# The mLSTM of a two-layer block: sums in four column groups of TensorE, state in row groups

## The chip, the cores and the metric

The kernel runs on one core of a Trainium2 chip, as one launch. The metric is the device time in microseconds, the median of several runs. A core has five engines that matter here: TensorE (PE in the profile, with its weight loads shown apart as PEld), VectorE (DVE), ScalarE (ACT), GpSimd (POOL) and SyncE (SP, which issues DMAs). Each engine works through its own list of instructions in order and waits on semaphores for the others.

## The reference

The input x has 4 sequences of 512 positions and 256 features. Layer 0 adds to x, both computed from the layer norm of x, an xLSTM block (an mLSTM and an MLP of 1024) and an FFN of 704 with low-rank experts. Layer 1 adds an attention and a sparsified FFN. Everything is in 32-bit floats. The change touches the mLSTM alone. It has 8 heads, with queries and keys of 16 and values of 32 numbers:

```python
logfg = jax.nn.log_sigmoid(f_pre)
Fcum = jnp.cumsum(logfg, axis=-1)
Dmat = Fcum[..., :, None] - Fcum[..., None, :] + i_pre[..., None, :]
Dmat = jnp.where(causal, Dmat, -jnp.inf)
m = jnp.max(Dmat, axis=-1, keepdims=True)
Smat = jnp.exp(Dmat - m)
qk = jnp.einsum('bhsd,bhtd->bhst', q, k) / jnp.sqrt(jnp.float32(dqk))
C = qk * Smat
n = jnp.maximum(jnp.abs(jnp.sum(C, axis=-1, keepdims=True)), jnp.exp(-m))
h = jnp.einsum('bhst,bhtd->bhsd', C / n, v)
```

So for every position two sums over the earlier positions are wanted, with the same weights C: the sum of C times the values (32 numbers a head) and the sum of C itself (one number a head).

## The kernel before

The 512 positions are cut into four stages j of 128 positions, all four sequences b together. The sum over earlier positions is split: within the stage it is computed from C, and what came before is carried in a state (key times value, summed over positions, faded from stage to stage). Each stage's mLSTM (`mlstm(j)`, L643) goes through these steps:

- Queries and keys come as 128 rows (8 heads of 16) by 512 columns (4 sequences of 128 positions).
- **h_ps** (L700, stages 1 to 3): what the old state gives. For each b, one matrix product with the queries as stationary operand (128 by 128) and the state of b as moving operand: 8 heads of 33 numbers, 264 columns. Each head uses only the rows of its own 16; the rest of the state is kept at zero by the mask `own_head`. ACT copies it to `hr`, positions on the partitions.
- **pass_on** (L786, stages 0 to 2) is the making of the new state: keys are transposed (`kt_ps`), and for each b one product `st_ps` of keys (stationary, 128 by 128) with weighted values (264 moving columns). DVE masks it with `own_head` and adds it to the state, which POOL has faded (L834).
- **ct** holds the exponents: for each head parity s, a tile [128 source positions, 4 head pairs r, 4 sequences of 128 target positions], so head 2r + s. It comes by DMA, POOL masks it, DVE subtracts, ACT takes the exponential.
- **qk** (L852): queries times keys, each in a row group of 32 rows of TensorE's array, four heads at once, each into its own PSUM bank; DVE multiplies it into `ct`, which is then C transposed.
- **weighted** (L814) is the sum within the stage. For each head and b one product **hp**: C of 128 by 128 as stationary operand, and as moving operand the 33 columns of `va`, 32 of the values and one with a factor, which gives the sum of C. DVE adds it to `hr`. There are 32 such products in a stage: 8 heads by 4 sequences.
- After that `hr` is normalised (L886 on) and goes through the output projection.

Every 32-bit product is two records in the profile, each a weight load and a matmul; a transpose is one record.

What runs when is set while the program is built. The generators (`experts`, `mlp`, `mlstm`, `routing` and so on) are streams. A planner (`Clock` L51, `Flow` L223) keeps an estimate of when each tile is ready and when each engine is free, and at each step lets the stream go on whose next product is ready; `flow.wait` names tiles and the number of free PSUM banks needed, `banks=4` for four. The order that comes of this is fixed in the program for every engine. So around the steps of the mLSTM stand products of the FFN (chunk, acc, gp, up, yp), and a change of one step moves others. All engine calls go through one helper, so nearly every row of the profile shows line L216, and rows are told apart by their tiles. `mm(..., at_once=4)` (L293) only tells the planner that four such products run side by side.

## Time and profile before

| | |
|---|---|
| median of 3 runs | 789.7 us (789.66 to 790.86) |
| the profiled execution, its own time | 789.78 us |
| its span, first to last instruction | 788.1 us, granted TensorE clock 1.000 |
| PE busy | 774.3 us (98%), 3334 records |
| DVE, ACT, POOL busy | 404.1, 265.1, 167.5 us |
| hp, h_ps, st_ps on PE | 256, 24, 24 records |

The span is what the trace covers; 1.7 us of the execution lie outside it. A PE record's duration in a group reaches from its start to the end of its result, and records overlap, so what a product costs a full engine is the distance from its start to the next start. A timeline row gives the first start, the time to the last end and the count of a run of equal records.

### The profile page before, as it was taken

Reading aid. Unit: us, or ns where it says so; the run is one execution under the profiler, and the core shown is the slowest. Engines: PE = TensorE matmul, PEld = TensorE weight load, DVE = VectorE, ACT = ScalarE, POOL = GpSimd, SP = SyncE. Lnnn points to the kernel's source line nnn. Section 1 sums busy time; section 2 is a strip of 40 time slices with the busy share of each in tenths; the row PEclk is TensorE's granted clock in tenths of the full one; section 3 lists DMA queues with packets and bytes.
Section 4 is the critical chain, followed back from the end, with each engine's and each line's share of the span. In section 5 each row is a group of like instructions: output and inputs, shape, how many; then the busy total and the mean of one; then the engine's idle time right before and its main releaser. Section 6 shows DMA issues by size and latency. Waiting matters only on the chain.

```text
span 788.1 us, 8741 instructions
## 1 busy us (share of the span) xinstructions
PE 774.3 (98%) x3334; PEld 531.5 (67%) x3334; DVE 404.1 (51%) x933; ACT 265.1 (34%) x473; POOL 167.5 (21%) x156
## 2 busy tenths in 40 slices
PE   6999999999999999999999999999999999999998
PEld 3687787867757787674778775656645485764487
DVE  4566545674331775432246532311278784836980
ACT  3536316471112564303146212011243405135310
POOL 5230250600240330140021031000333303233000
PEclk9999999999999999999999999999999999999999
DMA  8820001200000300000030121001000000000000
GB/s 257 268 95 1 0 1 36 73 1 1 0 1 0 109 1 1 1 1 0 0 108 1 44 75 44 0 1 53 0 1 0 1 27 1 1 27 1 0 22 33
DMA packets 18970, 25.37 MB, mean 32 GB/s; under 512 B 2800, under 2 KB 12784, under 8 KB 18928
## 3 DMA queue, kind: packets, MB, share of 16 engines
q1 hardware_dynamic: 17408, 24.39, 9.7%
q10 hardware_dynamic: 1520, 0.43, 0.2%
q8 instruction: 26, 0.43, 0.2%
q14 instruction: 16, 0.13, 0.1%
HBM read 22.65 MB, written 2.16 MB: 31 GB/s over the span
## 4 chain that ended last, share of the span: by engine, by line
PE 97%; ACT 1%; DMA 1%; DVE 0%; issue 0%
PE chunk L216 20%; PE yp L216 18%; PE gp L216 14%; PE up L216 14%; PE acc L216 11%; PE qk_ps L216 3%; PE hp L216 3%; PE vp L216 2%; PE pt L216 2%; PE o_ps L216 2%; PE lp L216 2%; PE v_ps L216 2%; PE qk L216 1%; PE k_ps L216 1%; PE q_ps L216 1%; PE h_ps L216 1%
## 5 line engine op out<-in xcount | busy, mean ns | idle before, releaser
L216 PE MATMUL chunk<-low,lora 128*128 128x256 f32 (+1 forms) x384 | 87.6, 385 | 1.6 <-DVE hid L216 1.0
L216 ACT ACTIVATE sl<-chunk 128x256 f32<-128x256 f32 x132 | 48.4, 385 | 107.7 <-PE chunk L216 98.9
L216 PE MATMUL chunk<-xnT,wguT 128*128 128x256 f32 (+1 forms) x384 | 84.2, 383 | 0.0
L216 PEld LDWEIGHTS chunk<-xnT,wguT 128*128 128x128 f32 (+1 forms) x384 | 63.6, 181 | 19.0 <-issue 7.4
L216 PEld LDWEIGHTS chunk<-low,lora 128*128 128x128 f32 (+1 forms) x384 | 63.0, 181 | 16.7 <-issue 4.8
L216 ACT ACT_TABLE_LOAD x46 | 59.0, 1283 | 11.4 <-DMA wvg<-in_WrT 6.1
L216 PE MATMUL gp<-featT,w_gate 128*128 128x512 f32 x128 | 60.3, 593 | 0.0
L216 PE MATMUL gp<-xnT,wguT 128*128 128x512 f32 x128 | 60.2, 592 | 0.0
L216 PE MATMUL up<-featT,w_up 128*128 128x512 f32 x128 | 60.2, 592 | 0.0
L216 PE MATMUL up<-xnT,lora 128*128 128x512 f32 x128 | 60.1, 592 | 0.0
L216 DVE TENSOR_TENSOR hid<-up,tmp 128x512 f32<-128x512 f32 x32 | 22.1, 692 | 72.7 <-PE up L216 70.0
L216 PE MATMUL yp<-w_down,hid 128*128 128x256 f32 x256 | 56.2, 379 | 0.0
L216 PE MATMUL yp<-w_gate,hs 128*128 128x256 f32 x256 | 56.2, 379 | 0.0
L216 PEld LDWEIGHTS yp<-w_down,hid 128*128 128x128 f32 x256 | 48.5, 190 | 8.2 <-issue 1.7
L216 PEld LDWEIGHTS yp<-w_gate,hs 128*128 128x128 f32 x256 | 48.6, 190 | 6.6
L216 ACT ACTIVATE tmp<-gp 128x512 f32<-128x512 f32 x32 | 19.1, 598 | 94.1 <-PE gp L216 94.1
L216 DVE TENSOR_TENSOR x<-yp,x 128x512 f32<-128x512 f32 (+1 forms) x18 | 11.4, 632 | 67.5 <-PE yp L216 67.5
L216 PEld LDWEIGHTS up<-xnT,lora 128*128 128x128 f32 x128 | 24.2, 190 | 29.3 <-issue 28.2
L216 PEld LDWEIGHTS up<-featT,w_up 128*128 128x128 f32 x128 | 24.2, 190 | 27.9 <-issue 27.3
L216 PEld LDWEIGHTS gp<-featT,w_gate 128*128 128x128 f32 x128 | 24.1, 190 | 27.9 <-issue 27.0
L216 PEld LDWEIGHTS gp<-xnT,wguT 128*128 128x128 f32 x128 | 24.1, 190 | 27.9 <-issue 27.3
L216 PE MATMUL acc<-WdT,hid 128*128 128x256 f32 (+1 forms) x192 | 41.5, 386 | 0.0
(198 smaller groups left out, 1209.4 us busy)
## 6 DMA issues: line engine op xcount, KB each, us to landing
ct<-m_dram SPq DMA_DIRECT2D x8, 1024.0 KB, 8.0
x<-in_x SPq DMA_DIRECT2D x3, 512.0 KB, 9.8
out<-x SPq DMA_DIRECT2D x6, 256.0 KB, 2.1
w_gate<-in_w_gate SPq DMA_DIRECT2D x1, 1024.0 KB, 6.7
w_up<-in_w_up SPq DMA_DIRECT2D x1, 1024.0 KB, 8.1
w_down<-in_w_down SPq DMA_DIRECT2D x1, 1024.0 KB, 11.2
wguT<-in_f_gate SPq DMA_DIRECT2D x1, 1024.0 KB, 5.0
lora<-in_f_up SPq DMA_DIRECT2D x1, 1024.0 KB, 4.8
```

What stands on the lines that cost most here:

```text
L216: return tc.keep_in_program_order(f(*args, **kw))
```

## The change

Two things are done to the mLSTM of layer 0.

The sums within the stage change operands. The values (32 columns of one head) become the stationary operand, in one of four column groups of the array, one for each head pair r; C becomes the moving operand, 128 columns. The result `hv` has head pair and value on the partitions and the target position along the row. The column with the factor is no longer part of it: a second set of products, `sums`, has as stationary operand 32 columns of the tile `ones_at`, zero but for one column at place s, so that the sums of all 8 heads of all sequences gather in one bank over both parities. ACT copies the three banks (two `hv`, one `sums`) into free parts of `ct`; `tok`, 12 transposes a stage, brings them back to positions on partitions, and DVE adds these three to `hr`.

The state is kept by row groups of two heads: 32 rows, with the values of two heads (66 columns) for each b, and the mask `parity` in place of `own_head`. `h_ps` is then 16 products a stage in four row groups, into four banks (`banks=4`), `st_ps` 16 products in four column groups, into one bank. One POOL instruction fades the whole state, with a factor that two small DVE instructions (`own`, `fade`) choose for each row; one DVE instruction masks it and one adds it.

```diff
-        state = [new(wk0, [P, H, DV + 1], f"state{b}") for b in range(B)]
+        state = new(wk0, [P, B, 2, DV + 1], "state")
+        ones_at = new(sm, [P, B, 2 * DV], "ones_at")
+        pool.memset(ones_at, 0.0)
...
             if not first:
+                yield from flow.wait(qs, state, banks=H // 2)
+                hps = [mm_ps("h_ps") for _ in range(H // 2)]
                 for b in range(B):
-                    yield from flow.wait(qs, state[b], banks=1)
-                    h_ps = mm_ps("h_ps")
-                    mm(h_ps[:, 0:W], qs[:, cols_of(b)], state[b].rearrange("p h d -> p (h d)"),
-                       start=True, stop=True)
-                    act.copy(hr[:, b, :, :], by_head(h_ps[:, 0:W]))
+                    for r, h_ps in enumerate(hps):
+                        mine = slice(32 * r, 32 * r + 32)
+                        mm(h_ps[:, b * W2 : (b + 1) * W2], qs[mine, cols_of(b)],
+                           state[mine, b, :, :].rearrange("p i d -> p (i d)"), start=True,
+                           stop=True, at_once=4)
+                for r, h_ps in enumerate(hps):
+                    act.copy(hr[:, :, 2 * r : 2 * r + 2, :],
+                             h_ps[:, 0 : B * W2].rearrange("p (b i d) -> p b i d", b=B, i=2))
...
+                st_ps = mm_ps("st_ps")
                 for b in range(B):
-                    mm(st_ps[:, 0:W], k_tok[:, b, :], wvs[b].rearrange("p h d -> p (h d)"),
-                       start=True, stop=True)
-                    dve.tensor_tensor(
-                        state[b] if first else wvs[b], by_head(st_ps[:, 0:W]), own_head, ALU.mult)
+                    for r in range(H // 2):
+                        mine = slice(32 * r, 32 * r + 32)
+                        mm(st_ps[mine, b * W2 : (b + 1) * W2], k_tok[:, b, mine],
+                           wvs[b][:, 2 * r : 2 * r + 2, :].rearrange("p i d -> p (i d)"),
+                           start=True, stop=True, at_once=4)
+                dve.tensor_tensor(
+                    new_state, st_ps[:, 0 : B * W2].rearrange("p (b i d) -> p b i d", b=B, i=2),
+                    parity.unsqueeze(1).unsqueeze(3).to_broadcast([P, B, 2, DV + 1]), ALU.mult)
...
-            def weighted(s, r):
-                hp = mm_ps("hp")
-                for b in range(B):
-                    mm(hp[:, b * (DV + 1) : (b + 1) * (DV + 1)], ct[s][:, r, cols_of(b)],
-                       va[:, b, 2 * r + s, :], start=True, stop=True)
...
+            def by_columns(out, lhsT, s, start, stop):
+                for b in range(B):
+                    for r in range(H // 2):
+                        mm(out[32 * r : 32 * r + 32, cols_of(b)], lhsT(b, r),
+                           ct[s][:, r, cols_of(b)], start=start and b == 0, stop=stop,
+                           at_once=4, skip_group_check=True)
+            def to_tokens(n):
+                yield from flow.wait(hvT[n], banks=1)
+                tok = mm_ps("tok")
+                for b in range(B):
+                    transpose(tok[:, cols_of(b)], hvT[n][:, cols_of(b)], ident)
...
+            for s in range(2):
+                yield from flow.wait(ct[s], banks=1 if sums else 2)
+                hv = mm_ps("hv")
+                by_columns(hv, lambda b, r: va[:, b, 2 * r + s, 0:DV], s, True, True)
+                if not sums:
+                    sums = mm_ps("sums")
+                    clock.held.add(sums.tensor.name)
+                by_columns(sums, lambda b, r: ones_at[:, b, DV - s : 2 * DV - s], s, s == 0, s == 1)
+                act.copy(hvT[s], hv)
+                if s == 1:
+                    act.copy(hvT[2], sums)
+                    clock.held.discard(sums.tensor.name)
+            for n in range(3):
+                yield from to_tokens(n)
```

The order of the changed program shows, in each of the four stages: both `qk` blocks, some products of the FFN, then `hv`, `sums`, `hv`, `sums` as one unbroken block of 64 products, then the three groups of `tok`, with products of the FFN between them in stages 0 and 2 and next to each other in stages 1 and 3.

More of the change, by code (lines that the diff above doesn't have):

```diff
@@ L403, in layers_kernel @@
     )
-    own_head = new(const, [P, H, DV + 1], "own_head")
-    nc.gpsimd.memset(own_head, 1.0)
-    for base, step in ((0, -DQK), (DQK - 1, DQK)):
+    own_pair = new(const, [P, H // 2], "own_pair")
+    nc.gpsimd.memset(own_pair, 1.0)
+    for base, step in ((0, -2 * DQK), (2 * DQK - 1, 2 * DQK)):
         nc.gpsimd.affine_select(
-            out=own_head, in_=own_head, pattern=[[step, H], [0, DV + 1]], compare_op=ALU.is_ge,
+            out=own_pair, in_=own_pair, pattern=[[step, H // 2]], compare_op=ALU.is_ge,
             fill=0.0, base=base, channel_multiplier=1 if step < 0 else -1)
@@ L475, in layers_kernel @@
         HB = H * B
-        W = H * (DV + 1)
+        W2 = 2 * (DV + 1)
         def tmp():
@@ L772, in mlstm @@
             carry["all"] = m_all
+            if sub_n is not None:
+                own = new(sm, [P, B, 2, H // 2], "own")
+                dve.tensor_tensor(
+                    own, dec[:, sub_n, :, :].rearrange("p (r i) b -> p b i r", i=2),
+                    own_pair.unsqueeze(1).unsqueeze(1).to_broadcast([P, B, 2, H // 2]), ALU.mult)
+                fade = new(sm, [P, B, 2], "fade")
+                dve.tensor_reduce(fade, own, AX.X, ALU.add)
             def spread_dec(n, b):
@@ L793, in pass_on @@
                 act.copy(k_tok, kt_ps.rearrange("p (b c) -> p b c", c=P))
+                yield from flow.wait(*wvs, k_tok, banks=1)
+                st_ps = mm_ps("st_ps")
                 for b in range(B):
-                    yield from flow.wait(wvs[b], k_tok, banks=1)
-                    st_ps = mm_ps("st_ps")
-                    mm(st_ps[:, 0:W], k_tok[:, b, :], wvs[b].rearrange("p h d -> p (h d)"),
-                       start=True, stop=True)
-                    dve.tensor_tensor(
-                        state[b] if first else wvs[b], by_head(st_ps[:, 0:W]), own_head, ALU.mult)
+                    for r in range(H // 2):
[3 more added lines that the diff above has]
+                           start=True, stop=True, at_once=4)
+                new_state = state if first else wvs[0].rearrange("p (b i) d -> p b i d", b=B)
+                dve.tensor_tensor(
+                    new_state, st_ps[:, 0 : B * W2].rearrange("p (b i d) -> p b i d", b=B, i=2),
+                    parity.unsqueeze(1).unsqueeze(3).to_broadcast([P, B, 2, DV + 1]), ALU.mult)
                 while not first and not faded:
                     yield flow.soon()
-                for b in range(B):
-                    if not first:
-                        yield from flow.wait(state[b])
-                        yield flow.spare()
-                        dve.tensor_tensor(state[b], state[b], wvs[b], ALU.add)
+                if not first:
+                    yield from flow.wait(state)
+                    yield flow.spare()
+                    dve.tensor_tensor(state, state, new_state, ALU.add)
                 passed.add(j)
@@ L811, in mlstm @@
                 flow.add(pass_on(), 1)
-            def weighted(s, r):
-                hp = mm_ps("hp")
-                for b in range(B):
-                    mm(hp[:, b * (DV + 1) : (b + 1) * (DV + 1)], ct[s][:, r, cols_of(b)],
-                       va[:, b, 2 * r + s, :], start=True, stop=True)
-                got = hp[:, 0 : B * (DV + 1)].rearrange("p (b d) -> p b d", b=B)
-                to = hr[:, :, 2 * r + s, :]
-                if first:
-                    dve.tensor_copy(to, got)
-                else:
-                    dve.tensor_tensor(to, got, to, ALU.add)
             for s in range(2):
@@ L833, in mlstm @@
             if not first:
-                for t, n in ((hr, old_n), (state, sub_n))[: 1 if last else 2]:
-                    for b in range(B):
-                        mine = t[b] if t is state else hr[:, b, :, :]
-                        pool.tensor_tensor(out=mine, in0=mine, in1=spread_dec(n, b), op=ALU.mult)
-                        yield flow.soon(0.6)
+                for b in range(B):
+                    mine = hr[:, b, :, :]
+                    pool.tensor_tensor(out=mine, in0=mine, in1=spread_dec(old_n, b), op=ALU.mult)
+                    yield flow.soon(0.6)
+                if not last:
+                    by_row = state.rearrange("p b i d -> p (b i) d")
+                    pool.tensor_tensor(
+                        out=by_row, in0=by_row, in1=fade.rearrange("p b i -> p (b i)").unsqueeze(
+                            2).to_broadcast([P, 2 * B, DV + 1]), op=ALU.mult)
                 faded.add(j)
@@ L849, in mlstm @@
                 act.activation(ct[s], ct[s], AF.Exp, scale=-1.0)
+            dve.tensor_copy(ones_at[:, :, DV], rr[:, 0, :])
+            sums = None
+            hvT = [ct[0][:, 2, :], ct[0][:, 3, :], ct[1][:, 0, :]]
+            def by_columns(out, lhsT, s, start, stop):
[7 more added lines that the diff above has]
+                tok = mm_ps("tok")
+                for b in range(B):
+                    transpose(tok[:, cols_of(b)], hvT[n][:, cols_of(b)], ident)
+                tok = tok.rearrange("p (b r d) -> p b r d", b=B, d=DV)
+                heads = hr.rearrange("p b (r s) d -> p b r s d", s=2)
+                if n < 2:
+                    got, to = tok, heads[:, :, :, n, 0:DV]
+                else:
+                    got, to = tok[:, :, :, 0:2], heads[:, :, :, :, DV]
+                if first:
+                    dve.tensor_copy(to, got)
+                else:
+                    dve.tensor_tensor(to, got, to, ALU.add)
             for s in range(2):
@@ L859, in mlstm @@
                     dve.tensor_tensor(ct[s][:, r, :], qk, ct[s][:, r, :], ALU.mult)
-                for r in range(H // 2):
-                    yield from flow.wait(ct[s][:, r, :], banks=1)
-                    weighted(s, r)
-                    yield flow.soon(0.4)
+            for s in range(2):
[12 more added lines that the diff above has]
+                yield from to_tokens(n)
             if first:
```

## The prediction

> **What bounds the kernel now.** I read the page's busy times first, then its chain, then who waits on TensorE.

> ```profile
> PE 774.3 (98%) x3334; PEld 531.5 (67%) x3334; DVE 404.1 (51%) x933; ACT 265.1 (34%) x473; POOL 167.5 (21%) x156
> ...
> PE   6999999999999999999999999999999999999998
> ...
> PE 97%; ACT 1%; DMA 1%; DVE 0%; issue 0%
> ```

> A busy PE is not yet a PE at its peak, but the chain that ended last is PE for 97% of the span. The list of PE's waits confirms it:

> ```profile
> PE pt L216 <- DVE xn L216: 5.8, 2, 5.6
> PE hp L216 <- DVE ct L216: 1.5, 2, 0.8
> PE vp L216 <- ACT xnT L216: 1.5, 1, 1.5
> PE chunk L216 <- DVE hid L216: 1.0, 2, 0.8
> PE chunk L216 <- DVE tmp L216: 0.6, 1, 0.6
> ```

> That is almost all of it: 10.6 us, of which 7.3 belong to the first 9 us. So the kernel is a queue of TensorE products with other work hidden behind it: what is saved on PE comes off the end, and what is saved elsewhere is worth nothing unless PE waits for it.

> **What a product costs.** This I take from start to next start, in the PE timeline.

> ```profile
> 36.08 0.60 PE L216 MATMUL kt_ps<-ident,kT 128*128 128x128 f32 x4
> 36.52 1.89 PE L216 MATMUL chunk<-xnT,wguT 128*128 128x256 f32 x8
> 38.25 1.94 PE L216 MATMUL st_ps<-wv,qs 128*128 128x264 f32 x8
> 40.03 1.89 PE L216 MATMUL chunk<-low,lora 128*128 128x256 f32 x8
> ```

> Full array: 256 moving columns cost 1.73/8 = 0.216 us a record, 264 columns 1.78/8 = 0.223, a transpose 0.44/4 = 0.109. So a moving column costs 0.84 ns, and 128 of them 0.107 us.

> ```profile
> 22.29 1.95 PE L216 MATMUL chunk<-xnT,wguT 128*64 128x256 f32 x16
> ...
> 63.83 0.59 PE L216 MATMUL acc<-tmp,lora 128*128 128x512 f32 x1
> 64.35 1.17 PE L216 MATMUL qk<-qm,kT 32*128 32x128 f32 x32
> 66.29 1.08 PE L216 MATMUL hp<-va,ct 128*128 128x33 f32 x8 [0.76 <-DVE ct L216]
> 67.20 1.19 PE L216 MATMUL vp<-wvg,xnT 128*128 128x280 f32 x4
> 68.23 0.97 PE L216 MATMUL hp<-va,ct 128*128 128x33 f32 x8
> 69.04 2.13 PE L216 MATMUL vp<-wvg,xnT 128*128 128x280 f32 x8
> ```

> hp: 8 records from 66.29 to 67.20 and from 68.23 to 69.04, 0.91 and 0.81 us, 0.10 to 0.11 a record though only 33 columns move (28 ns): the load of 128 stationary columns is the price.
> qk, four row groups: 32 records in 1.17 us, the last lasting 0.27, so 0.90 from the first start to the last. That is 8 rounds of four; the first round also pays a load of weights that nothing hides (0.1), and a round costs 0.80/7 = 0.114, by single records 0.111. Four products thus take the time of one of 128 columns: four really run at once.
> Two column groups (first row, 128 rows by 64 columns): last record 0.38 long, 1.57 us for 7 intervals of two products, 0.224: again the time of one.
> Changing the tiling of the array: the one acc before qk takes 0.52, while 512 columns take 0.43 (q_ps, two in 0.86). So 0.09 to enter, the same to leave (h_ps before a two-column chunk: 8 records 1.88, less 8 x 0.223), and the first load uncovered, 0.1 for 128 stationary columns, about 0.03 for 32.

> **The change part by part.** *Removed on PE.* hp: 128 products, 256 records, 32 groups of 8 at 0.81 to 0.91, mean 0.83: 26.6 us. h_ps and st_ps: 24 records each at 0.223: 5.35 + 5.35. The two waits for ct before hp, 1.5: they come because each hp group follows its qk at once; in the new order products lie between. Together 38.8 us.

> *Added on PE.* hv and sums: 128 products each, 512 records, in rounds of four: 128 rounds. Each moves 128 columns and loads four times 32. No row shows four column groups; the bounds are 0.107 (all four at once, loads hidden) and 4 x 0.107 = 0.43 (one after the other). Nearest rows are qk (four tiles, other direction) and the two-column chunk (this direction, two tiles); both come out at the time of one. I take 0.111: 14.2 us. sums costs as much as hv, though it brings one number a head.
> tok: 48 transposes at 0.109: 5.2.
> h_ps: 96 records, 24 rounds; 66 columns move (55 ns), but 128 stationary columns are loaded as in qk: 0.111, 2.7 us.
> st_ps: 24 rounds of 66 moving and 32 stationary columns, between 0.055 (moving) and 0.111; I take 0.062, near the moving bound since the load is short: 1.5.
> Changes of tiling: four blocks of hv at 0.12 in and 0.2 out, three of st_ps likewise, three of h_ps at about 0.33 (two of them run into a two-column chunk): 1.3 + 1.0 + 1.0 = 3.3.
> Together 26.9 us, so 11.9 less.

> [...]

> [...] Here four row groups give 4 x 0.107/0.111 = 3.86. [...]

> *Other engines, hidden.* DVE loses 32 additions or copies of hr (mean 0.295, 9.4 us) and 20 state instructions (0.43, 8.6); it gains 8 of 128x512 from PSUM (0.69, like hid from up), 5 on the state, 12 tiny ones of about 0.2: some 8 less. POOL loses 8 fades of 0.636 and gains 2. ACT gains 12 copies of 0.59, 7 us on an engine busy 34%. No DMA is added or moved. All this lies behind PE's 98% and counts nothing.

> *New waits.* The second hv needs all of the second ct. In stage 0, the tightest, two chunk products follow qk (1.0 us with the change of tiling), then 0.12, then hv and sums of the first parity, 16 rounds or 1.8 us: PE arrives 3.0 us after the last qk start. DVE's four multiplications end 2.8 us after it (they took 2.48 from 0.28 on). In the other stages 1.7 to 3.4 us of products lie between. tok waits for ACT: the third group comes 1.1 us after the last sums (0.2 out of tiling, eight transposes), the copy needs 0.3 + 0.6. So both are covered, with about 0.2 to spare; if DVE or ACT is behind with FFN work, each stage waits that long, up to some 1 us. Behind a waiting hv stand the FFN products of the same queue. I allow 0.2 in all.

> **The sum.** Profiled span 788.1 - 11.9 + 0.2 = 776.4; the execution was 1.7 longer, 789.78, which is the median but for 0.1: 789.7 - 11.7 = 778.0.

> **The rivals.**
> [...]
> (2) *Waits in place of work*: hv late on DVE's ct, tok on ACT, in all stages 0.5 to 1.2 us each, 2 to 5 given back: 780 to 783. For it: the margins above; before, hp waited twice for ct. Against: DVE and ACT have slack there, and PE waited for little else.
> (3) *Two column groups at once at most, slower than before*: here four different moving streams of 128 rows each have to be read, and the row shows two. A round then costs 0.222, 152 rounds 16 us more: 794. The change breaks even at 11.7/152 = 77 ns over my value, 0.188 a round. Against: four row groups show no such limit, but they read a quarter of the rows each.
> (4) *The change does not do what it says*, the products fall apart into single ones: the built order has them round after round, hv and sums as one block of 64 a stage, so only the array itself can do this; that is (3) or worse.

> **How the numbers follow.** The forecast 68% (its own range 776 to 780), (1) 13%, (2) 11%, (3) and (4) 7%, a rest of 1%. The range 775.5 to 785 holds the forecast, (2) and most of (1), and leaves out (3). Within 0.2% (1.6 us, about what a measurement of this kernel can tell from no change) lies only a narrow strip between (1) and (3): 2%. Faster 90%, slower 8%.

> **What would show it.** [...] tok 0.109 a transpose. h_ps and st_ps under 1 us a stage against 1.8 before. PE's waits: no hp; hv for ct or tok for ACT each under 0.5 in sum; if over 2, it is (2). PE busy about 764. The granted clock stays 1.0. A wait of PE in the FFN or in layer 1 that is not there now would make the prediction wrong in a way that I have not priced.

## The result, and the profile after

| | before | after |
|---|---|---|
| median, six executions each | 790.3 us (789.66 to 790.86) | 785.12 us (784.47 to 786.74) |
| profiled execution, its span | 789.78, 788.1 us | 784.47, 782.6 us |
| granted TensorE clock | 1.000 | 0.996 |

The ratio is 0.9938 (95% interval 0.9925 to 0.9951). The change makes the kernel 5.2 us faster, where 11.7 were forecast.

The page of the kernel after, its busy times, two rows of its slices and its chain:

```profile
PE 765.3 (98%) x3782; PEld 516.3 (66%) x3782; DVE 397.7 (51%) x906; ACT 270.1 (35%) x485; POOL 166.2 (21%) x151
...
PE   6999999999999998999999999999999999999998
...
PEclk9999999999999998999999999999999999999999
...
PE 92%; DVE 3%; ACT 2%; issue 1%; DMA 1%; ACTq 0%; DVEq 0%
```

PE's busy time fell by 9.0 us, but the chain is no longer PE from end to end: 97% became 92%, and DVE and ACT stand in it with 5% where there was 1. And one slice (the sixteenth, 293 to 313 us) has an 8 in both rows: there PE had gaps, and there its clock was not full. PE's waits (engine and tile, what it waited for: us in all, times, the longest):

```profile
PE pt L216 <- DVE xn L216: 5.8, 2, 5.6
PE chunk L216 <- DVE tmp L216: 5.6, 4, 3.7
PE vp L216 <- ACT xnT L216: 1.4, 1, 1.4
PE vp L216 <- DVE tmp L216: 0.8, 1, 0.8
```

The first and third are those of before. hp's 1.5 us are gone, and so is most of the wait for `hid`; in their place PE waits for DVE's `tmp` 5.6 us instead of 0.6, of which one wait is 3.7.

**The products themselves.** PE timeline of the kernel after (first start, time to the last end, records): a `st_ps`, the block of `hv` and `sums` in stage 0, and an `h_ps`.

```profile
37.75 0.67 PE L216 MATMUL st_ps<-wv,qs 128*32 128x66 f32 x32
38.35 1.99 PE L216 MATMUL chunk<-low,lora 128*128 128x256 f32 x8
...
75.57 1.08 PE L216 MATMUL hv<-ct,va 128*32 128x128 f32 x32
76.47 1.06 PE L216 MATMUL sums<-ct,ones_at 128*32 128x128 f32 x32
77.34 1.06 PE L216 MATMUL hv<-ct,va 128*32 128x128 f32 x32
78.22 1.06 PE L216 MATMUL sums<-ct,ones_at 128*32 128x128 f32 x32
79.20 0.66 PE L216 MATMUL tok<-ident,ct 128*128 128x128 f32 x4
...
129.29 1.12 PE L216 MATMUL h_ps<-state,qs 32*128 32x66 f32 x32
130.34 1.99 PE L216 MATMUL chunk<-xnT,wguT 128*128 128x256 f32 x8
```

From 75.57 to 79.20 are 3.63 us for 32 rounds of four: 0.113 with the way in and out of the tiling, 0.109 from round to round by single records. Four column groups on the same rows do run at once, with their loads hidden (a round takes 0.109, 128 moving columns alone 0.107). A `st_ps` takes 0.60, an `h_ps` 1.05.

**Where the time went.** I gave every PE record the time from its start to the next start, waits included, and summed it by tile in both traces. The mLSTM's products: 37.9 us before (hp 27.1, h_ps 5.5, st_ps 5.3), 25.8 after (hv 7.1, sums 7.4, tok 5.4, h_ps 3.2, st_ps 2.7, in which 0.87 is a wait of the product behind it). That is 12.2 less, by the unrounded sums. All other products together take 6.8 *more*, though none was added: chunk from `low` alone 7.2, acc from `tmp` 0.9, while qk lost 0.75 (1.67 less, since hp's waits had counted there, and 0.92 more, of which below). So the saving was made, and over half of it was lost again in FFN products that the change doesn't touch.

**The place.** The PE timeline of the kernel after in stage 2; the last bracket is the idle time before the group and what ended it:

```profile
289.96 1.89 PE L216 MATMUL chunk<-xnT,wguT 128*128 128x256 f32 x8
291.70 1.13 PE L216 MATMUL chunk<-low,lora 128*128 128x256 f32 x4
296.56 2.08 PE L216 MATMUL chunk<-low,lora 128*128 128x256 f32 x4 [3.73 <-DVE tmp L216]
298.57 2.09 PE L216 MATMUL qk<-qm,kT 32*128 32x128 f32 x32
300.59 1.65 PE L216 MATMUL acc<-tmp,lora 128*128 128x512 f32 x2
```

PE stands still for 3.73 us. Afterwards four chunk records take 2.01 us to the next start (0.96 in the rows of other places, with the change of tiling), qk 2.02 instead of 1.10, the two acc 1.58 instead of some 0.95: another 2.6 us. The reason for the second part is in the windows (a stretch, its length, busy time of PE, PEld, DVE, ACT and POOL, granted clock, DMA):

```profile
294.50:295.00 0.50, 0.00 (x0) 0.00 (x0) 0.00 (x0) 0.50 (x1) 0.00 (x0) 0.86 0.00 0
295.00:295.50 0.50, 0.00 (x0) 0.00 (x0) 0.00 (x0) 0.50 (x1) 0.00 (x0) 0.50 0.00 0
297.00:301.00 4.00, 4.00 (x37) 2.94 (x37) 0.32 (x1) 0.38 (x1) 0.00 (x0) 0.50 0.02 4
...
301.50:302.00 0.50, 0.50 (x2) 0.00 (x0) 0.50 (x2) 0.00 (x0) 0.00 (x0) 0.81 0.00 0
```

The clock is granted at half from 294.86 (0.36 us of that slice at 1.0, the rest at 0.5, gives 0.86) to 301.69, 6.83 us.

What PE waited for stands in ACT's timeline at the same place:

```profile
290.48 0.66 ACT L216 ACTIVATE sl<-chunk 128x256 f32<-128x256 f32 x2
291.15 1.28 ACT L216 ACT_TABLE_LOAD   x1
292.45 1.91 ACT L216 ACTIVATE ct<-ct 128x2048 f32<-128x2048 f32 x1
294.37 1.28 ACT L216 ACT_TABLE_LOAD   x1
295.67 1.21 ACT L216 ACTIVATE sl<-chunk 128x256 f32<-128x256 f32 x4
```

The chain of the experts' FFN is chunk on PE, `sl` on ACT, `tmp` on DVE, the second half of chunk on PE. Between two `sl` stands here the exponential of the mLSTM's second `ct`, with a load of a function table before it and one after it: 1.28 + 1.91 + 1.28 = 4.5 us in which ACT gives the FFN nothing. Before, ACT had the same hole, and PE had work in it:

```profile
292.50 1.28 ACT L216 ACT_TABLE_LOAD   x1
293.79 1.91 ACT L216 ACTIVATE ct<-ct 128x2048 f32<-128x2048 f32 x1
295.73 1.28 ACT L216 ACT_TABLE_LOAD   x1
297.02 1.22 ACT L216 ACTIVATE sl<-chunk 128x256 f32<-128x256 f32 x4
```

```profile
292.70 1.02 PE L216 MATMUL acc<-tmp,lora 128*128 128x512 f32 x2
293.56 1.89 PE L216 MATMUL chunk<-xnT,wguT 128*128 128x256 f32 x8
295.28 1.89 PE L216 MATMUL chunk<-low,lora 128*128 128x256 f32 x8
```

So the theory: the planner, given a shorter mLSTM, lays the streams differently against each other; in stage 2 the products that would have covered ACT's hole had been issued already, PE runs dry, and the idle stretch also costs the full clock. A count of the records in the two traces agrees. When ACT's hole begins (292.50 before, 291.15 after), PE has issued 252 records of chunk from `low`, 264 of chunk from `xnT` and 44 of acc from `tmp` in the kernel before, but 260, 278 and 48 in the kernel after. Those 26 records are some 6.5 us of PE's work (an estimate from 0.216 a chunk and 0.43 an acc), more than the hole's 4.5. That this lead is what emptied the queue is argued from the count, not shown by a run.

### The profile page after: what moved, and what is told of

It is laid out like the page before. It is cut to its first block, busy times and chain, and to the rows that moved or that the text cites. A ratio compares the mean times of both kernels' runs of the same rounds, so it can differ in the third digit from the quotient of the medians.

```text
span 782.6 us, 9629 instructions
## 1 busy us (share of the span) xinstructions
PE 765.3 (98%) x3782; PEld 516.3 (66%) x3782; DVE 397.7 (51%) x906; ACT 270.1 (35%) x485; POOL 166.2 (21%) x151
## 4 chain that ended last, share of the span: by engine, by line
PE 92%; DVE 3%; ACT 2%; issue 1%; DMA 1%; ACTq 0%; DVEq 0%
PE yp L216 18%; PE chunk L216 17%; PE up L216 14%; PE gp L216 14%; PE acc L216 10%; PE qk_ps L216 4%; PE vp L216 2%; PE pt L216 2%; PE v_ps L216 2%; PE o_ps L216 2%; PE lp L216 2%; ACT L216 1%; PE qk L216 1%; PE hv L216 1%; PE sums L216 1%
## 5 line engine op out<-in xcount | busy, mean ns | idle before, releaser
L216 PE MATMUL chunk<-low,lora 128*128 128x256 f32 (+1 forms) x384 | 89.3, 389 | 6.1 <-DVE tmp L216 5.6
L216 ACT ACTIVATE sl<-chunk 128x256 f32<-128x256 f32 x132 | 48.5, 385 | 107.6 <-PE chunk L216 90.0
L216 PE MATMUL chunk<-xnT,wguT 128*128 128x256 f32 (+1 forms) x384 | 84.4, 384 | 0.0
L216 PEld LDWEIGHTS chunk<-low,lora 128*128 128x128 f32 (+1 forms) x384 | 63.0, 182 | 23.9 <-DVE tmp L216 7.0
L216 PEld LDWEIGHTS chunk<-xnT,wguT 128*128 128x128 f32 (+1 forms) x384 | 63.6, 181 | 22.1 <-issue 9.2
L216 DVE TENSOR_TENSOR hid<-up,tmp 128x512 f32<-128x512 f32 x32 | 22.1, 692 | 84.3 <-PE up L216 77.8
L216 PE MATMUL up<-featT,w_up 128*128 128x512 f32 x128 | 60.2, 592 | 0.0
L216 PE MATMUL gp<-xnT,wguT 128*128 128x512 f32 x128 | 60.2, 592 | 0.0
L216 PE MATMUL up<-xnT,lora 128*128 128x512 f32 x128 | 60.2, 592 | 0.0
L216 PE MATMUL gp<-featT,w_gate 128*128 128x512 f32 x128 | 60.1, 592 | 0.0
L216 PE MATMUL yp<-w_gate,hs 128*128 128x256 f32 x256 | 56.2, 379 | 0.0
L216 ACT ACTIVATE tmp<-gp 128x512 f32<-128x512 f32 x32 | 19.1, 597 | 107.3 <-PE gp L216 107.3
L216 PE MATMUL yp<-w_down,hid 128*128 128x256 f32 x256 | 56.1, 379 | 0.0
L216 PEld LDWEIGHTS yp<-w_down,hid 128*128 128x128 f32 x256 | 48.6, 190 | 8.3 <-issue 1.4
L216 PEld LDWEIGHTS yp<-w_gate,hs 128*128 128x128 f32 x256 | 48.6, 190 | 6.6
L216 DVE TENSOR_TENSOR x<-yp,x 128x512 f32<-128x512 f32 (+1 forms) x18 | 11.3, 630 | 66.6 <-PE yp L216 66.6
L216 PEld LDWEIGHTS up<-xnT,lora 128*128 128x128 f32 x128 | 24.2, 190 | 29.3 <-issue 28.2
L216 POOL TENSOR_TENSOR pd<-k,q 128x256 f32<-128x256 f32 (+3 forms) x16 | 25.2, 1574 | 83.2 <-ACT k L216 83.2
L216 PEld LDWEIGHTS gp<-xnT,wguT 128*128 128x128 f32 x128 | 24.1, 190 | 27.9 <-issue 27.3
L216 PEld LDWEIGHTS gp<-featT,w_gate 128*128 128x128 f32 x128 | 24.2, 190 | 27.6 <-issue 27.0
L216 PEld LDWEIGHTS up<-featT,w_up 128*128 128x128 f32 x128 | 24.0, 190 | 27.8 <-issue 27.0
```

Source lines behind the costliest of these rows:

```text
L216: return tc.keep_in_program_order(f(*args, **kw))
```

## The experiments

The theory says that the products' saving of some 12 us is there in any order, and that the rest is order and clock. Its rivals: the new products themselves slow down what runs beside them, so that the loss comes back wherever the order is moved; or one of the two parts of the change carries it. In the text below, "front" is the work that opens the next stage (layer norm `xn`, its transposes `pt`, `vp`, keys and queries), which `following` starts.

**The front later, in both kernels.** The due time at which the planner starts the next stage's front is moved; no computation changes.

```diff
         def following(j):
-            yield flow.soon(30)
+            yield flow.soon(36)
```

> The changed kernel, but the next stage's front (layer norm, transposes, vp) starts 36 us after the stage instead of 30; every instruction is kept, only their order moves, so that other products stand where TensorE waited 3.9 us at 292. Theory A (the products cost what was forecast; 7 us were lost in that one wait and in the half clock of 6.8 us behind it): 785.1 - 3.9 - 2.7 = 778.5, 777 to 780.5, granted clock 1.000, no wait of PE for DVE's tmp over 1.5 us after the first 10 us. Theory B (ACT and DVE can't keep up with the shorter PE queue; the wait only moves): 783 to 786, with 4 us or more of such waits elsewhere.

> The kernel before, with the same later front and nothing else. Theory A: it has no long wait to remove, so the time stays within 1.5 us of 790. Theory C (a later front is better whatever the mLSTM does, and has nothing to do with the change): 783 to 786.

Measured: after with the later front 783.07 us (781.29 to 784.26), ratio to before 0.9909 [0.9891, 0.9928]; before with the later front 790.02 (789.3 to 790.89), ratio 1.0000 [0.9991, 1.0009]. The order as such is worth nothing to the kernel before and 2 us to the one after, less than the full recovery that the theory set at 778.5; the time lies in the range of theory B, which said that the wait only moves, though not with B's 4 us of such waits (2.0 for `tmp` in all). In the trace (of the fastest execution, 781.29) the wait at 292 is gone, the mLSTM's products are 13.0 down, but 4.5 are lost elsewhere, the longest single piece in one new wait (PE timeline of after with the later front):

```profile
149.69 0.55 PE L216 MATMUL pt<-ident,xn 128*128 128x128 f32 x3
151.92 0.77 PE L216 MATMUL pt<-ident,xn 128*128 128x128 f32 x5 [1.69 <-DVE xn L216]
```

Moving the order closed one hole and opened another. That speaks for order, but doesn't yet exclude the first rival.

**Each part alone.** One kernel has only `hv`, `sums` and `tok`, with the state as before; the other only the state by row groups, with hp as before.

```diff
# columns alone: before, with
-                for r in range(H // 2):
-                    yield from flow.wait(ct[s][:, r, :], banks=1)
-                    weighted(s, r)
+            for s in range(2):
+                yield from flow.wait(ct[s], banks=1 if sums else 2)
+                by_columns(hv, lambda b, r: va[:, b, 2 * r + s, 0:DV], s, True, True)
...
# state alone: after, with
-                by_columns(hv, lambda b, r: va[:, b, 2 * r + s, 0:DV], s, True, True)
...
+                for r in range(H // 2):
+                    yield from flow.wait(ct[s][:, r, :], banks=1)
+                    weighted(s, r)
```

> The kernel before with the first part alone: hv, sums and tok in place of hp; the state as before (own_head is stored once a head and broadcast, to make room). Forecast's own terms: 28.1 off, 20.7 on, so 7.4 less than before: 783, if its order holds no wait over 2 us. Theory A: 782 to 785, hv and sums 0.111 a round. Theory D (the column groups cost more than they show in their own rows, through contention with the FFN): 787 or more.

> The kernel before with the second part alone: state, h_ps and st_ps in row and column groups; hp as before. The products alone: 10.7 off, 6.2 on, 785.8. Its order has, near 293, the same shape as the changed kernel's (chunk products with nothing ready between them). Theory A: there PE waits about 4 us and loses its full clock again, 789.5 to 792.5, so no gain. Theory E (the wait comes from hv and tok): 785 to 787, no such wait.

Columns alone: 785.26 us (784.62 to 786.27), ratio 0.9940 [0.9925, 0.9955]. Its products are 7.1 down and everything else 2.9 up, without a loss of clock; 2.3 above the 783 expected, just beyond the range given. State alone: 795.77 (795.13 to 796.14), ratio 1.0071 [1.0056, 1.0086], *slower* than before, and outside what was expected, though its products are 5.7 down as they should be. The other products are 11.8 up. PE timeline of the state alone:

```profile
150.59 0.33 PE L216 MATMUL pt<-ident,xn 128*128 128x128 f32 x1 [0.31 <-DVE xn L216]
152.60 0.77 PE L216 MATMUL pt<-ident,xn 128*128 128x128 f32 x5 [1.69 <-DVE xn L216]
...
304.11 2.07 PE L216 MATMUL chunk<-low,lora 128*128 128x256 f32 x4 [3.73 <-DVE tmp L216]
```

It has the very wait of the full change (3.73, for `tmp`, and four chunk records that take 2.07 us together behind it, 2.08 in after) *and* the one at 150, there with 3.4 us at half clock. This kernel has no `hv`, `sums` or `tok`, so these don't make the wait: as far as it blames them, the first rival falls. The state's own products are left to suspect.

**The state alone, with the later front.** The same edit of one number on that kernel.

> The second part alone (state in row and column groups) with the later front; same instructions as the run of the second part alone, other order. Theory A (that run lost its 5.7 us of products and 6 us more to two waits with half clock): 790.3 - 5.7 + 0 to 2 = 784.6 to 786.6. Theory F (the row and column groups of the state disturb something that follows them in any order): 790 or more.

788.34 us (785.84 to 790.28), ratio 0.9977 [0.9962, 0.9992]: 7.4 us back from an edit of order. In the trace the other products are 2.1 up in place of 11.8, so the state's products in themselves don't slow what stands beside them. The median still lies above the 784.6 to 786.6 of theory A. The ten executions form two groups, five at 785.84 to 787.25 with clock 1.000 and five at 789.43 to 790.28 with 0.996 (the profiled one is of the first). What dropped the clock in the others no trace shows.

**Keep PE busy in the hole.** The order of after stays, and where PE would wait at 292, 16 products (32 records) with 128 columns of `ones_at` that are all zero are added into a bank that is still open. The edit sits where the planner finds no product ready, so it had left this stretch idle itself. The zeros change no sum and leave the wait for `tmp` as it is. If idle time costs only itself, this gains nothing.

```diff
         def idle(self, t, why=""):
             if t > self.now:
+                if 290.4 < self.now < 291.5 and self.open is not None and not self.warmed:
+                    self.warmed = True
+                    for _ in range(16):
+                        pe.matmul(self.open[:, 0:P], ident, ones_at[:, :, 0:DV], start=False,
+                                  stop=False, skip_group_check=True)
...
+                    flow.open = dps[half] if c < last - 1 else None
```

> The changed kernel in its own order, with 16 products of zeros (128 moving columns, 3.5 us by the transposes' and hp's pitch) added to an open acc bank in the wait of 3.9 us near 292; they add zero and come while PE waits anyway. Theory A1 (the half clock of 6.8 us follows from the idle TensorE): the wait stays, the clock stays 1.000, 785.1 - 2.7 = 782.4, 781.5 to 783.5. Theory A2 (the clock falls for another reason): 784.5 to 786, clock 0.996 again.

782.26 us (782.1 to 782.97), ratio 0.9902 [0.9888, 0.9917]: 2.9 us faster than after, by adding work. PE timeline and one window of this kernel:

```profile
292.95 3.73 PE L216 MATMUL acc<-ones_at,ident 128*128 128x128 f32 x32
296.85 1.13 PE L216 MATMUL chunk<-low,lora 128*128 128x256 f32 x4 [0.16 <-DVE tmp L216]
297.91 1.17 PE L216 MATMUL qk<-qm,kT 32*128 32x128 f32 x32
```

```profile
296.50:303.30 6.80, 6.64 (x54) 4.20 (x53) 4.72 (x12) 1.19 (x5) 0.00 (x0) 1.00 0.01 2
```

The chunk starts at the same place behind `tmp`, the four records now take 1.06 to the next start in place of 2.01, and qk 1.10 in place of 2.02. So the half clock comes from PE's idling, and costs 2.9 of the 6.8.

**How much idling is enough?** The same kernel with 8 and with 4 such products, so that 2 and 3 us of the wait stay empty.

> As the run with 16 products of zeros in the wait near 292, but with 8: they end 1.9 us after the wait begins, so TensorE is idle for 2.0 us in place of 3.9. Theory G (the full clock is lost only by an idle stretch near 3 us or longer): clock 1.000 and 782 to 783 in every execution. Theory H (about 2 us are enough when they fall badly): some executions near 782.3 at clock 1.000 and some near 785 at 0.996.

> The same with 4 products of zeros: 3.0 us idle are left. Theory G: the clock falls in every execution or in most, 784.5 to 786.5. Theory H: most executions fall, 784.5 to 786.5, some stay at 782.5.

With 8: 782.39 us (781.91 to 783.54), ratio 0.9904 [0.9889, 0.9918], the clock 1.000 in all four executions. With 4: 785.27 (782.28 to 786.0), ratio 0.9931 [0.9909, 0.9953]; three of the four at 0.996 to 0.997, one (782.28) at 1.000. The chunk behind the wait, of the one with 8 and then of the one with 4:

```profile
298.11 1.13 PE L216 MATMUL chunk<-low,lora 128*128 128x256 f32 x4 [1.95 <-DVE tmp L216]
```

```profile
297.68 2.08 PE L216 MATMUL chunk<-low,lora 128*128 128x256 f32 x4 [2.84 <-DVE tmp L216]
```

1.95 us of idling was free of the penalty in four executions of four, 2.84 in one of four, 3.73 in none of the six of after.

**Both edits of the order together.** If ACT's hole is what PE runs into, the two exponentials of a stage can be put together, so that one pair of table loads serves both. With the later front this was expected to bring the forecast's time.

```diff
-            yield flow.soon(30)
+            yield flow.soon(36)
...
                         c, c, g.unsqueeze(3).to_broadcast([P, 2, B, P]), ALU.subtract)
-                yield from flow.wait(ct[s])
+            yield from flow.wait(*ct)
+            for s in range(2):
                 act.activation(ct[s], ct[s], AF.Exp, scale=-1.0)
```

> The changed kernel with the later front (36 us), and both exponentials of a stage's ct one after the other on ACT, once both tiles are ready, so that Silu work isn't stopped twice by two table loads; every other instruction is kept. Theory A (the products save 12 us; what was given back is waits that the order of the streams makes): 790.3 - 12.2 + 0 to 1.5 = 778 to 779.6, PE's waits after the first 10 us no more than before's 3 us, clock 1.000. Theory B (the shorter queue can't be fed): 782 to 785.

778.38 us (777.97 to 778.46), ratio 0.9851 [0.9836, 0.9865]: the fastest of all, 6.7 us below after. Its waits of PE, but for those of before:

```profile
PE vp L216 <- DVE ct L216: 0.8, 1, 0.8
PE chunk L216 <- DVE tmp L216: 0.6, 1, 0.6
PE chunk L216 <- DVE he_pair L216: 0.3, 1, 0.3
...
PE hv L216 <- DVE ct L216: 0.2, 1, 0.2
```

The wait for `tmp` is at the 0.6 of before, the clock at 1.000, the mLSTM's products 12.1 down, all others 0.7 up. ACT's hole has not gone: with both exponentials in it, it is 6.3 us long (292.70 to 299.02). But PE passes it with acc and chunk, and behind it has products of another stream, the MLP's gp and up. One row of ACT and two of PE from this kernel:

```profile
294.00 3.71 ACT L216 ACTIVATE ct<-ct 128x2048 f32<-128x2048 f32 x2
...
298.69 1.88 PE L216 MATMUL gp<-featT,w_gate 128*128 128x512 f32 x4
300.40 1.88 PE L216 MATMUL up<-featT,w_up 128*128 128x512 f32 x4
```

**Is it the edits and not the change?** The same two edits on the kernel before.

> The kernel before with the same two edits (later front, both exponentials together). Theory A: no long wait to remove, 789 to 791.5. Theory C (these edits are the gain, whatever the mLSTM does): 784 to 787.

792.33 us (791.42 to 793.03), ratio 1.0026 [1.0016, 1.0035]: there they *cost* 2.3 us, beyond what either expectation named. The trace shows 3.1 us in all, spread over vp, chunk, kt_ps, up and gp, and no single wait over 0.8 that before has not; why, I can't say. So the edits are no gain in themselves; only with the shorter mLSTM do they fit.

**The exponentials without the later front.** If ACT's table loads alone were the cause, this edit alone should heal it.

> The changed kernel with both exponentials together, but the front at 30 us as it was: the second half of the two edits that gave 778.4. Its order again has chunk products with nothing ready between them near 293. Theory A: the wait of about 4 us and the half clock come back there, 784 to 788. Theory I (putting the exponentials together is the cure, since it spares table loads on ACT): 778 to 780.

788.81 us (788.41 to 789.91), ratio 0.9989 [0.9979, 0.9998]: nearly all of the saving is lost, more than any expectation allowed. Products 12.0 down, all others 10.7 up. Its PE timeline:

```profile
75.79 3.51 PE L216 MATMUL qk<-qm,kT 32*128 32x128 f32 x32 [0.65 <-DVE ct L216]
...
301.45 2.08 PE L216 MATMUL chunk<-low,lora 128*128 128x256 f32 x4 [3.81 <-DVE tmp L216]
```

The hole on ACT is one and longer (two exponentials, 3.71 us, between the two table loads: 6.3 us), PE has again nothing else at that moment, and in stage 0 waits for ACT's `va` (0.67) and DVE's `ct` (0.65) in qk are followed by another loss of the clock (0.92 in the mean from 73 to 79 us, 0.70 from 79 to 83). So neither edit is a cure. What counts is whether a stream with ready products stands beside the hole.

Four orders of the changed kernel, then, by the due time of the front and the place of the exponentials:

| | front at 30 | front at 36 |
|---|---|---|
| exponentials apart | 785.12 | 783.07 |
| exponentials together | 788.81 | 778.38 |
| mLSTM's products against before | -12.2, -12.0 | -13.0, -12.1 |
| all others against before | +6.8, +10.7 | +4.5, +0.7 |

(The last two rows give apart, together.) The saving is the same in all four within 1.1 us; the order takes between 0.7 and 10.7 of it back.

## Why the prediction was wrong

The direction was right, and so were the prices of the products; the sum missed by 7 us, in one term.

- *A round of four column groups costs 0.111*: right, 0.109 by single records and 0.113 over a block; the first load of 32 columns, set at 0.03, took 0.024 (a first round of 0.133). The rival with two groups at once (0.222) is out. So is rival (1), dearer rounds from loads not hidden (13%, most of it inside the range): no run shows its price, and what the runs showed in its place is the 0.109. Four column groups of the same 128 rows gave 4 x 0.107/0.109 = 3.93, four row groups 3.86.
- *tok at 0.109 a transpose*: 5.41 for 48, 5.2 forecast. *h_ps and st_ps*: 1.05 and 0.60 a stage (without the wait behind one st_ps), forecast with their tiling 1.2 and 0.8. *hp and the rest removed*: 37.9 against 37.3. Together the mLSTM's products gave 12.2, where the working without waits had 10.4; the changes of tiling cost less than I had set. (The 0.09 to enter a tiled block, ten times, stands in the product before it and so among the others' 6.8; the 0.87 of wait in st_ps makes up for it.) That these 1.8 us came on top was luck, and hid a part of the loss.
- *The other engines, hidden*: their busy time came out near the forecast (DVE 6 us less, ACT 5 more), but see below.
- *hv late for ct, tok late for ACT*: neither waited. The margins that I worked out held.
- *The clock stays 1.0*: wrong, 0.996.
- ***New waits, "I allow 0.2 in all"*: this is the step that failed.** I asked only whether the new instructions would wait, and not whether the old ones still had their cover. In a kernel whose order is planned, 12 us less of one stream means that the others meet ACT's queue at other moments: with less mLSTM between them, the FFN's products were 26 records further on when ACT's hole came. In place of the 0.2 all other products took 6.8 us more: one FFN wait of 3.7 us, 2.6 to 2.9 for the clock, and the balance of small waits and changes of tiling. "What is saved on PE comes off the end" holds only as long as PE has something ready at each moment. The rival "waits in place of work" had the right kind and the wrong place: the waits came in the FFN, which I had named as unpriced. I could have read the danger before: ACT's four-and-a-half-microsecond holes between `sl` and `sl` stand in the trace of before, and the changed order says what PE has to do beside them.

Shown by runs: that the saving is in the products (every order), that order moves the loss (later front, exponentials), that the wait does not need `hv`, `sums` and `tok` (state alone), that idling costs the clock (zeros in the hole). Read from two traces only: that the table loads and the second exponential were what `sl` waited for; the one run that moves them alone moved the hole and did not remove it. Open: what dropped the clock in part of the executions of the two kernels with the later front and the exponentials apart (two of four of after, five of ten of the state alone), and why the kernel before loses 2.3 us to the two edits.

## What to carry to other kernels

When a change takes work from a busy engine, look for what that work was holding apart: list the long holes of the other engines' queues (here a table load, an exponential, a table load, 4.5 us) and ask what the busy engine will have ready beside each in the new order. Measure the saving in the changed products by themselves, start to start, apart from the span; if it is there and the span doesn't show it, the order is what to work on, and edits that are worth nothing or a loss by themselves (0 and -2.3 us on the kernel before) can be worth 6.7 us. Where PE stood still for 3.73 us here, 16 products that change nothing were 2.9 us cheaper than the clock that it lost, 8 of them 2.7; 4 left the median where it was (785.27 against 785.12).

## What was unexpected of the hardware

The loss after the fall comes out by halves: of the 6.83 us in after PE stood idle for the first 1.70, and half of the other 5.13 is 2.57, near the 2.6 of the rows.

**Four tiles in either direction.** Weight loads of 128 rows by 32 columns into one column group lay under the products of the three others but for 0.002 us (0.109 a round, 0.107 for the moving columns alone); nothing before had shown more than two column groups.
